# Transposes on the two halves of the TensorE array's rows in a fused encoder-decoder kernel

## The chip, the core and the metric

The kernel runs on one core of one Trainium2 chip. The metric is device time in microseconds (us) of one launch. Before the change three runs took 2826.58, 2827.00 and 2828.27 us; their median is 2827.0 us.

## The reference

A context of 77 rows goes through an encoder layer, and two sequences of 2048 rows go through a decoder layer (width 512, 16 heads of 32, hidden width 2048), all in fp32:

```
x = src
x = x + mha(ln(x), ln(x), ..., eb)
x = x + relu(ln(x) @ ff1.T + b1) @ ff2.T + b2
y = tgt
y = y + mha(ln(y), ln(y), ..., sb)        # causal, 2048 x 2048, 16 heads, two sequences
y = y + mha(ln(y), x, ..., cb)            # cross, 2048 x 77
y = y + relu(ln(y) @ ff1.T + b1) @ ff2.T + b2

scores = einsum('bhqd,bhkd->bhqk', q, k) / sqrt(32) + bias
attn = softmax(scores)
out = einsum('bhqk,bhkd->bhqd', attn, v)
```

The decoder's causal self-attention is most of the first 1745 us; the cross attention and the feed-forward layer of the decoder fill the rest.

## The kernel before

**Order.** Every engine has one queue, and each runs its instructions in the order in which the program emits them; there is no scheduler, the order is written out by hand. An engine that waits for a semaphore holds everything behind it.

**Units.** A unit is one sequence `b` (0, 1), one block `m` of 512 query rows (0 to 3), one group `g` of four heads (0 to 3) and one tile `t` of 128 rows (0 to 3): 128 units, in that order. Tile number `i = 4m + t` attends to `i + 1` key tiles, cut by `pieces` into pieces of two to four key tiles.

**One unit.** `scores` (L376) multiplies, for one piece, the four heads of the group on the four 32-row strips of the array, into four PSUM banks. VectorE copies each bank to SBUF and takes its maximum (L385; the diagonal with its bias, L392). After the last piece VectorE forms the negated maximum `nm` (L402), and the four exponentials of the unit, one for each head (ScalarE, L407), are put on a list, `late_exps`, from which `exps(k)` emits the next `k`. `turn` takes one or two pieces of a unit and transposes each 128x128 tile of the probabilities with TensorE (L428): four tiles to a PSUM bank, and one copy of that bank to the SBUF buffer `pts_all`. The first half of the banks of a turn is copied by ScalarE (L434), the second half by VectorE (L432); in the first block (m = 0) they take turns. After the fourth bank `turn` emits one exponential of a later unit, after the last another one. `values` (L445) multiplies the transposed tiles by V, on four column strips, into PSUM bank 7.

**The loop.** For each pair of pieces the main loop emits: the turn; after the last pair of a unit, `slot` (projections of q, k, v, the output projection, parts of the next block's normalization, here called jobs: L215, L226, L239, L251, each with eight matmuls over one bank; the transposes of a normalized tile, L308, and of the reciprocals of the softmax sums, L464); one piece of scores of a later unit, one to three exponentials; the values; and more scores where they may run ahead (up to two units).

**Banks.** `bank()` hands out seven PSUM banks in rotation. An operation that takes the n-th bank waits until the (n-7)-th has been read.

**Second part.** From 1745 us on eight blocks of 512 rows run through cross attention and feed-forward (matmuls L1323, L1352, L1424). There `bank()` rotates over four banks, `turned` of `attend_stages` transposes the 16 heads' probabilities of a tile (L814, four banks, ScalarE copies at L815), and `turned` of `norm_stages` four tiles of 128x128 (L759).

A matmul in fp32 stands in the trace as two passes, each with its weight load (PEld); a transpose as one. The lines that the steps below touch:

Of the kernel before, what the change touches and what calls it, by code (L numbers as in the profile page):

```python
# [11 lines left out]
AF = mybir.ActivationFunctionType  # L12
ALU = mybir.AluOpType
# [4 lines left out]
P = 128  # L18
B, T, S, D = 2, 2048, 77, 512
H, HD, DFF = 16, 32, 2048  # L20
NC = D // P
NF = DFF // P
HC = P // HD
MB = 512
NMB = T // MB
TB = MB // P
EPS = 1e-6
# [27 lines left out]
def tile_encoder_decoder(ctx: ExitStack, tc: tile.TileContext, ins, out):  # L55
    nc = tc.nc
    x, src = ins["x"], ins["ctx_1024"]
# [10 lines left out]
    ident = const.tile([P, P], F32, name="ident")  # L68
# [89 lines left out]
    with (  # L158
# [6 lines left out]
        kT = ac.tile([P, NC, T], F32, name="kT")  # L165
# [4 lines left out]
        nTt = ac.tile([P, NC, MB], F32, name="nT")  # L170
        wbt = ac.tile([P, NC, D], F32, name="wbig")
        pts_all = ac.tile([P, 8, HC * P], F32, name="pts")
        oT_all = ac.tile([P, 6, TB * P], F32, name="oT")
        bv = ac.tile([P, D], F32, name="row_sa_bv")
        bo = ac.tile([P, D], F32, name="row_dec_sa_out_b")
        psum = ps.tile([P, 8, 512], F32, name="psum")
        count = {"bank": 0, "banks": 7, "pts": 0, "oT": 0, "mm": 0}

        def bank():

            i = count["bank"] % count["banks"]
            count["bank"] += 1
            return psum[:, i, :]

        def in_turn(what, tile):
# [112 lines left out]
        def norm_turn(b, m, t, apart=False):  # L298
            xn = xs.pop((b, m, t))
            if t == 0:  # L300
                nTs[b, m] = nTt
            nT = nTs[b, m]

            pts = [bank()] * NC
            if apart:
                pts[0] = bank()
            for c in range(NC):
                nc.tensor.transpose(pts[c][:, ts(c, P)], xn[:, ts(c, P)], ident)  # L308
            for c in range(NC):
                d, pt = nT[:, c, ts(t, P)], pts[c]  # L310
                sc, bi = vec("dec_n1_s", c), vec("dec_n1_b", c)
                if c or not apart:
                    nc.scalar.activation(d, pt[:, ts(c, P)], AF.Identity, bias=bi, scale=sc)  # L313
                else:
                    nc.vector.tensor_scalar(d, pt[:, ts(c, P)], sc, bi, ALU.mult, ALU.add)


        def pieces(i):
# [15 lines left out]
        state = {}  # L334
# [78 lines left out]
        def turn(pieces):  # L413

            first = units[pieces[0][0]][1] == 0
            by_head = first or units[pieces[0][0]][2:] == (0, 0)
            loads = []
            for n, k0, kn in pieces:
                ks = range(k0, k0 + kn)
                if by_head:  # L420
                    loads += [[(n, k, r) for k in ks] for r in range(HC)]
                else:
                    loads += [[(n, k, r) for r in range(HC)] for k in ks]
            for o, load in enumerate(loads):
                pt = bank()
                pts = in_turn("pts", pts_all).rearrange("p (x q) -> p x q", q=P)
                for x, (n, k, r) in enumerate(load):
                    nc.tensor.transpose(pt[:, ts(x, P)], state[n]["p"][r][:, ts(k, P)], ident)  # L428
                    got[n, k, r] = pts[:, x, :]
                w = len(load) * P  # L430
                if o % 2 if first else o >= (len(loads) + 1) // 2:
                    nc.vector.tensor_copy(pts[:, : len(load), :], pt[:, :w])  # L432
                else:
                    nc.scalar.copy(pts[:, : len(load), :], pt[:, :w])  # L434
                if o == min(3, len(loads) - 1):
                    exps(1)
            exps(HC if first else 1)

# [14 lines left out]
        def divide(b, m, g):  # L453


            ri = sm.tile([P, TB, HC], F32, name="ri", tag="ri", bufs=2)
            nc.vector.reciprocal(ri, sums_of[b, m, g])
            rows = sm.tile([P, TB, HC, HD], F32, name="rirows", tag="rirows", bufs=1)
            nc.vector.tensor_copy(rows, ri[:, :, :, None].to_broadcast([P, TB, HC, HD]))
            yield  # L460
            rb = bank()
            flat = rows.rearrange("p t r d -> p (t r d)")
            for t in range(TB):
                nc.tensor.transpose(rb[:, ts(t, P)], flat[:, ts(t, P)], ident)  # L464
            nc.vector.tensor_tensor(ots[b, m, g], rb, ots[b, m, g], ALU.mult)
            yield


# [266 lines left out]
        def norm_stages(y, n, row, place, done):  # L735

            keep = {}

            def stats():
                st = sm.tile([P, 6], F32, name="bnst", tag="bnst")  # L740
                mv = sm.tile([P, 2], F32, name="cmv", tag="cmv", bufs=4)
                rs = sm.tile([P, 3], F32, name="crs", tag="crs", bufs=4)
                nc.vector.bn_stats(st, y())
                nc.vector.bn_aggr(mv, st)
                nc.vector.tensor_scalar_add(rs[:, 0:1], mv[:, 1:2], EPS)
                nc.gpsimd.tensor_tensor(rs[:, 1:2], rs[:, 0:1], mhalf[:, 0:1], ALU.pow)
                nc.gpsimd.tensor_scalar(rs[:, 2:3], mv[:, 0:1], rs[:, 1:2], -1.0, ALU.mult, ALU.mult)
                keep.update(rs=rs)

            def center():  # L750
                xn = keep["xn"] = place()
                rs = keep["rs"]
                nc.scalar.activation(xn, y(), AF.Identity, bias=rs[:, 2:3], scale=rs[:, 1:2])
                nc.gpsimd.tensor_tensor(y(), y(), row, ALU.add)

            def turned():
                xn, pt, dst = keep["xn"], bank(), done()
                for c in range(NC):
                    nc.tensor.transpose(pt[:, ts(c, P)], xn[:, ts(c, P)], ident)  # L759
                for c in range(NC):  # L760
                    sc, bi = vec(f"dec_{n}_s", c), vec(f"dec_{n}_b", c)
                    nc.scalar.activation(dst[:, c, :], pt[:, ts(c, P)], AF.Identity, bias=bi, scale=sc)

            return stats, center, turned

# [6 lines left out]
        def attend_stages(q, kTc, v, y, biased, pr, pts, place, w_o, bi=None):  # L772


            prh = pr.rearrange("p (h k) -> p h k", k=S)
            by_r = pr.rearrange("p (g r k) -> p g r k", r=HC, k=S)
            keep = {}
# [30 lines left out]
                nc.gpsimd.tensor_tensor(prh, prh, ri[:, :, None].to_broadcast([P, H, S]), ALU.mult)  # L808

            def turned():  # L810
                for g in range(NC):
                    pt = bank()
                    for r in range(HC):
                        nc.tensor.transpose(pt[:S, ts(r, P)], prh[:, g * HC + r, :], ident)  # L814
                    nc.scalar.copy(pts(g), pt[:S, :])  # L815

            def times_v():
                ot = bank()
                for g in range(NC):
                    for r in range(HC):  # L820
                        h = g * HC + r
                        nc.tensor.matmul(  # L822
                            ot[rows4(r), ts(g, P)], v[:, ts(h, HD)], pts(g)[:, ts(r, P)], start=True, stop=True
                        )
                keep["oT"] = place()
                nc.scalar.copy(keep["oT"], ot)
# [9 lines left out]
        def first_cross():  # L836
# [7 lines left out]
            o = 2 * HC * MB  # L844
# [13 lines left out]
            def pts(g):  # L858
                return kT[:S, g, 2 * MB : 3 * MB]

            def loads():
                for t in range(TB):
# [581 lines left out]
        def cross(x):  # L1444
# [26 lines left out]
            for t in range(TB):  # L1471
                at = 14 + 7 * t
                y = lambda t=t: y_of(x, t)
                biased = m == 0 and t < 2
                fs = attend_stages(
                    lambda g, t=t: qT[g // 2][:, g % 2, ts(t, P)], kTcs[b], vcs[b][:S, :], y, biased, pr,
                    lambda g: pts_all[:S, g, :], place("xr"), wbt,
                    bias_1 if biased and t else None,
                )
# [129 lines left out]
```

## Time and profile before

| | |
|---|---|
| median of the runs | 2827.0 us |
| the profiled execution, span | 2828.5 us |
| TensorE busy (matmul records) | 2796.6 us, 99% |
| VectorE busy | 1872.9 us, 66% |
| ScalarE busy | 1454.0 us, 51% |
| GpSimd busy | 787.9 us, 28% |
| transposes at L428 | 4352, 536.6 us |
| self-attention, by the first scores of each block | 24.4 to about 1745 us |

The span is that of one execution under the profiler. A row of the timeline gives the start, the length, the engine, the line and the operation, the output and the inputs, the shapes and the count, and in brackets how long the engine had been idle and what ended that. The end of a matmul is modelled with its way through the array, so a TensorE that is shown busy can still have gaps: what one transpose costs in a row of them is read from the length of the row and its count, not from the mean of one. The DMA queues' packets take 38% of the time of the 16 DMA engines.

### The profile page before, as it was taken

Reading aid. Unit: us, or ns where it says so; the run is one execution under the profiler, and the core shown is the slowest. Engines: PE = TensorE matmul, PEld = TensorE weight load, DVE = VectorE, ACT = ScalarE, POOL = GpSimd, SP = SyncE. Lnnn points to the kernel's source line nnn. Section 1 sums busy time; section 2 is a strip of 40 time slices with the busy share of each in tenths; the row PEclk is TensorE's granted clock in tenths of the full one; section 3 lists DMA queues with packets and bytes.
Section 4 is the critical chain, followed back from the end, with each engine's and each line's share of the span. In section 5 each row is a group of like instructions: output and inputs, shape, how many; then the busy total and the mean of one; then the engine's idle time right before and its main releaser. Section 6 shows DMA issues by size and latency. Waiting matters only on the chain.

```text
span 2828.5 us, 65166 instructions
## 1 busy us (share of the span) xinstructions
PE 2796.6 (99%) x25950; PEld 2062.6 (73%) x25950; DVE 1872.9 (66%) x5288; ACT 1454.0 (51%) x2785; POOL 787.9 (28%) x697
## 2 busy tenths in 40 slices
PE   9899999999999999999999999999999999999998
PEld 5557666666666556666666677888888888888888
DVE  4666687778887577687878895464645555555545
ACT  3544466656666556656656676434344444444431
POOL 0200050200000201120100002282828283837356
PEclk9999999999999999999999999999999999999999
DMA  6414343401111412332401014463637464646466
GB/s 172 122 33 130 119 137 103 125 17 46 34 44 58 120 48 61 80 102 68 124 20 32 21 60 144 135 216 116 205 120 207 138 197 127 194 131 187 125 201 194
DMA packets 252642, 319.10 MB, mean 113 GB/s; under 512 B 29568, under 2 KB 142512, under 8 KB 252210
## 3 DMA queue, kind: packets, MB, share of 16 engines
q1 hardware_dynamic: 252338, 314.93, 37.7%
q8 instruction: 205, 3.36, 0.5%
q14 instruction: 99, 0.81, 0.1%
HBM read 274.91 MB, written 39.95 MB: 111 GB/s over the span
## 4 chain that ended last, share of the span: by engine, by line
PE 93%; DVE 3%; ACT 1%; issue 1%; DMA 1%; POOL 1%; SPq 0%; POOLq 0%; ACTq 0%; DVEq 0%
PE psum L428 17%; PE psum L1323 14%; PE psum L1352 12%; PE psum L376 11%; PE psum L445 9%; PE psum L215 4%; PE psum L831 4%; PE psum L251 4%; PE psum L239 4%; PE psum L226 3%; PE psum L1424 3%; PE psum L814 2%; DVE pp L385 1%; PE psum L784 1%; PE psum L822 1%; PE psum L546 1%
## 5 line engine op out<-in xcount | busy, mean ns | idle before, releaser
L407 ACT ACTIVATE pp<-pp,nm 128x128 f32<-128x128 f32 (+15 forms) x512 | 612.7, 1204 | 219.7 <-DVE nm L402 219.2
L385 DVE TENSOR_SCALAR_CACHE_REDUCE pp<-psum 128x512 f32<-128x512 f32 (+3 forms) x1024 | 559.4, 591 | 61.7 <-PE psum L376 60.2
L428 PEld LDWEIGHTS psum<-ident,pp 128*128 128x128 f32 x4352 | 472.9, 141 | 111.8 <-DVE pp L385 53.1
L428 PE MATMUL psum<-ident,pp 128*128 128x128 f32 x4352 | 536.6, 277 | 9.2 <-ACT pp L407 2.8
L434 ACT COPY pts<-psum 128x512 f32<-128x512 f32 (+3 forms) x598 | 298.8, 571 | 437.6 <-PE psum L428 333.4
L432 DVE COPY pts<-psum 128x512 f32<-128x512 f32 (+3 forms) x556 | 330.8, 648 | 68.6 <-PE psum L428 68.5
L376 PE MATMUL psum<-kT,q 32*128 32x512 f32 (+3 forms) x2560 | 356.6, 576 | 6.0 <-ACT nT L313 2.7
L445 PEld LDWEIGHTS psum<-pts,vv 128*32 128x32 f32 x8704 | 226.0, 110 | 123.9 <-issue 116.0
L1352 PEld LDWEIGHTS psum<-pp 128*128 128x128 f32 x2560 | 295.8, 192 | 17.4 <-issue 12.8
L1352 PE MATMUL psum<-pp 128*128 128x128 f32 x2560 | 306.4, 276 | 1.9 <-POOL pp L1105 1.6
L445 PE MATMUL psum<-pts,vv 128*32 128x128 f32 x8704 | 278.8, 275 | 0.7 <-ACT pts L434 0.5
L1105 POOL TENSOR_TENSOR pp<-pp 128x512 f32<-128x512 f32 x155 | 209.5, 1368 | 111.7 <-DMA pp<-in_dec_ff_wT_dram 90.8
L1323 PE MATMUL psum<-vv,pp 128*128 128x256 f32 x1024 | 238.5, 381 | 0.0
L376 PEld LDWEIGHTS psum<-kT,q 32*128 32x128 f32 x2560 | 122.9, 183 | 141.2 <-issue 87.9
L1323 PEld LDWEIGHTS psum<-vv,pp 128*128 128x128 f32 x1024 | 189.8, 190 | 26.3 <-issue 1.9
L392 DVE CUSTOM_DVE_ANT_0 pp<-psum,bias 128x256 f32<-128x256 f32 (+1 forms) x512 | 196.0, 411 | 17.0 <-PE psum L376 17.0
L285 POOL TENSOR_TENSOR rstd<-rstd,mhalf 128x1 f32<-128x1 f32 x32 | 18.2, 569 | 659.1 <-DVE rstd L284 608.6
L1336 DVE TENSOR_TENSOR kT<-kT,psum 128x512 f32<-128x512 f32 x96 | 65.7, 685 | 181.0 <-PE psum L1323 181.0
L1339 ACT ACTIVATE kT<-kT,vecs 128x256 f32<-128x256 f32 x192 | 86.9, 500 | 168.7 <-DVE kT L1336 168.1
L1323 PE MATMUL psum<-nT,pp 128*128 128x256 f32 x768 | 173.4, 379 | 0.0
L1323 PEld LDWEIGHTS psum<-nT,pp 128*128 128x128 f32 x768 | 145.3, 190 | 22.6 <-issue 3.5
L808 POOL TENSOR_TENSOR oT<-oT,cri 128x1232 f32<-128x1232 f32 x28 | 67.7, 2416 | 283.4 <-DVE cri L803 258.4
(193 smaller groups left out, 3724.5 us busy)
## 6 DMA issues: line engine op xcount, KB each, us to landing
pp<-w_d SPq DMA_DIRECT2D x520, 256.0 KB, 2.9
pp<-in_dec_ff_wT_dram SPq DMA_DIRECT2D x112, 256.0 KB, 4.0
wqk<-in_dec_sa_in_wT_dram SPq DMA_DIRECT2D x64, 256.0 KB, 4.0
bias<-tzg SPq DMA_DIRECT2D x128, 128.0 KB, 3.8
wbig<-in_dec_sa_in_wT_dram SPq DMA_DIRECT2D x8, 1024.0 KB, 6.4
vv<-in_enc_ff_wT_dram SPq DMA_DIRECT2D x8, 1024.0 KB, 5.2
wbig<-in_dec_sa_out_wT_dram SPq DMA_DIRECT2D x8, 1024.0 KB, 6.4
vv<-y SPq DMA_DIRECT2D x32, 256.0 KB, 5.1
```

The lines of the kernel that those rows point to most:

```text
L215: nc.tensor.matmul(mm, w[:, c, :], nTs[b, m][:, c, :], start=(c == 0), stop=(c == NC - 1))
L376: nc.tensor.matmul(banks[r][:, : kn * P], q[rows4(r), ts(t, P)], kT[rows4(r), g, k0 * P : (k0 + kn) * P], start=True, stop=True,)
L385: nc.vector.tensor_scalar(p[:, k0 * P : (k0 + far) * P], s[:, : far * P], 1.0, None, ALU.mult, ALU.max, accum_out=st["mx"][:, r, c : c + 1],)
L392: nc.vector.tensor_tensor_reduce(p[:, (i + 1) * P - w : (i + 1) * P], s[:, far * P : kn * P], biases[b, m, g][:, r, 2 * P - w :], 1.0, LOW ...
L407: nc.scalar.activation(p, p, AF.Exp, bias=nm, accum_out=to)
L428: nc.tensor.transpose(pt[:, ts(x, P)], state[n]["p"][r][:, ts(k, P)], ident)
L432: nc.vector.tensor_copy(pts[:, : len(load), :], pt[:, :w])
L434: nc.scalar.copy(pts[:, : len(load), :], pt[:, :w])
L445: nc.tensor.matmul(ot[rows4(r), t, :], vv[:, k, ts(g * HC + r, HD)], got.pop((n, k, r)), start=(k == 0), stop=(k == i),)
L1105: engine.tensor_tensor(out, a, b, ALU.subtract)
L1323: nc.tensor.matmul(mm[:, ts(f, TOK)], a[:, c, ts(f, P)], b[:, c, :], start=fresh and f == 0 and c == 0, stop=c == 1, skip_group_check=True,)
L1352: nc.tensor.matmul(psum[:, bank_i, ts(col, P)], lhs[:, c, :], w[:, c, :], start=fresh and k in (0, 3) and c == 0, stop=c == 3, skip_group_ ...
```

## The change

`turn_halves` replaces each 128x128 transpose by two: rows 0 to 63 of the tile on the upper half of the array's rows and rows 64 to 127 on the lower half. Each streams 64 columns of the identity and writes 64 columns of the output, the one into a first bank, the other into a second. `two_banks` hands out two banks of the rotation. A pair of banks so holds eight tiles, each bank the halves of all eight. `turn` puts two of its former loads of four tiles into one group, and both engines copy of every group: ScalarE the first bank, VectorE the second, eight runs of 64 columns each. One exponential is now emitted after the second group. `pts_all` is used as a ring of 32 tiles, from its start again where a turn doesn't fit. All other transposes of the decoder (L308, L464, L759, L814) are changed in the same way; those of the encoder stay.

```diff
+        def two_banks():
+            n = count["bank"]
+            count["bank"] += 2
+            i, j = sorted((n % count["banks"], (n + 1) % count["banks"]))
+            return psum[:, i : j + 1 : j - i, :]
+
+        def turn_halves(pt, x, src, width=P):
+            for a in range(2):
+                rows = slice(a * HALF, (a + 1) * HALF)
+                nc.tensor.transpose(pt[:width, a, ts(x, HALF)], src[rows], ident[rows, rows])
...
-            for o, load in enumerate(loads):
-                pt = bank()
-                pts = in_turn("pts", pts_all).rearrange("p (x q) -> p x q", q=P)
+            groups = [sum(loads[o : o + 2], []) for o in range(0, len(loads), 2)]
+            if count["pts"] + sum(map(len, groups)) > pts_ring.shape[1]:
+                count["pts"] = 0
+            for o, load in enumerate(groups):
+                pt, w = two_banks(), len(load)
+                pts = pts_ring[:, count["pts"] : count["pts"] + w, :]
+                count["pts"] += w
                 for x, (n, k, r) in enumerate(load):
-                    nc.tensor.transpose(pt[:, ts(x, P)], state[n]["p"][r][:, ts(k, P)], ident)
+                    turn_halves(pt, x, state[n]["p"][r][:, ts(k, P)])
                     got[n, k, r] = pts[:, x, :]
-                w = len(load) * P
-                if o % 2 if first else o >= (len(loads) + 1) // 2:
-                    nc.vector.tensor_copy(pts[:, : len(load), :], pt[:, :w])
-                else:
-                    nc.scalar.copy(pts[:, : len(load), :], pt[:, :w])
-                if o == min(3, len(loads) - 1):
+                for a, copy in enumerate((nc.scalar.copy, nc.vector.tensor_copy)):
+                    copy(
+                        pts[:, :, ts(a, HALF)], pt[:, a, : w * HALF].rearrange("p (x q) -> p x q", q=HALF)
+                    )
+                if o == min(1, len(groups) - 1):
                     exps(1)
             exps(HC if first else 1)
...
             def turned():
-                for g in range(NC):
-                    pt = bank()
-                    for r in range(HC):
-                        nc.tensor.transpose(pt[:S, ts(r, P)], prh[:, g * HC + r, :], ident)
-                    nc.scalar.copy(pts(g), pt[:S, :])
+                for g in range(0, NC, 2):
+                    pt = two_banks()
+                    for x in range(2 * HC):
+                        turn_halves(pt, x, prh[:, g * HC + x, :], S)
+                    d = pts.rearrange("p g (r a q) -> p g r a q", r=HC, a=2)[:, g : g + 2]
+                    for a in range(2):
+                        nc.scalar.copy(
+                            d[:, :, :, a, :], pt[:S, a, :].rearrange("p (g r q) -> p g r q", g=2, q=HALF)
+                        )
```

More of the change, by code (lines that the diff above doesn't have):

```diff
@@ L23 @@
 HC = P // HD
+HALF = P // 2
 MB = 512
@@ L302, in norm_turn @@
             nT = nTs[b, m]
-            pts = [bank()] * NC
+            pts = [two_banks()] * NC
             if apart:
-                pts[0] = bank()
+                pts[0] = two_banks()
             for c in range(NC):
-                nc.tensor.transpose(pts[c][:, ts(c, P)], xn[:, ts(c, P)], ident)
+                turn_halves(pts[c], c, xn[:, ts(c, P)])
             for c in range(NC):
-                d, pt = nT[:, c, ts(t, P)], pts[c]
+                d, pt = joined(nT[:, c, ts(t, P)]), pts[c][:, :, ts(c, HALF)]
                 sc, bi = vec("dec_n1_s", c), vec("dec_n1_b", c)
                 if c or not apart:
-                    nc.scalar.activation(d, pt[:, ts(c, P)], AF.Identity, bias=bi, scale=sc)
+                    nc.scalar.activation(d, pt, AF.Identity, bias=bi, scale=sc)
                 else:
-                    nc.vector.tensor_scalar(d, pt[:, ts(c, P)], sc, bi, ALU.mult, ALU.add)
+                    nc.vector.tensor_scalar(d, pt, sc, bi, ALU.mult, ALU.add)
         def pieces(i):
@@ L460, in divide @@
             yield
[L461 removed]
+            rb = two_banks()
             flat = rows.rearrange("p t r d -> p (t r d)")
             for t in range(TB):
[L464 to L465 removed]
+                turn_halves(rb, t, flat[:, ts(t, P)])
+            o = ots[b, m, g].rearrange("p (t a q) -> p a t q", t=TB, a=2)
+            nc.vector.tensor_tensor(
+                o, rb[:, :, : TB * HALF].rearrange("p a (t q) -> p a t q", q=HALF), o, ALU.mult
+            )
             yield
@@ L756, in turned @@
             def turned():
-                xn, pt, dst = keep["xn"], bank(), done()
+                xn, pt, dst = keep["xn"], two_banks(), done()
                 for c in range(NC):
-                    nc.tensor.transpose(pt[:, ts(c, P)], xn[:, ts(c, P)], ident)
+                    turn_halves(pt, c, xn[:, ts(c, P)])
                 for c in range(NC):
                     sc, bi = vec(f"dec_{n}_s", c), vec(f"dec_{n}_b", c)
-                    nc.scalar.activation(dst[:, c, :], pt[:, ts(c, P)], AF.Identity, bias=bi, scale=sc)
+                    nc.scalar.activation(
+                        joined(dst[:, c, :]), pt[:, :, ts(c, HALF)], AF.Identity, bias=bi, scale=sc
+                    )
             return stats, center, turned
@@ L822, in times_v @@
                         nc.tensor.matmul(
-                            ot[rows4(r), ts(g, P)], v[:, ts(h, HD)], pts(g)[:, ts(r, P)], start=True, stop=True
+                            ot[rows4(r), ts(g, P)], v[:, ts(h, HD)], pts[:, g, ts(r, P)], start=True, stop=True
                         )
```

9 lines of the change are left out of this document (6 added, 3 removed).

## The prediction

> **What bounds the kernel now.** I read the page first, then the table by stage, then the timeline of one turn in each kind of block.
>
> ```profile
> span 2828.5 us, 65166 instructions
> PE 2796.6 (99%) x25950; PEld 2062.6 (73%) x25950; DVE 1872.9 (66%) x5288; ACT 1454.0 (51%) x2785; POOL 787.9 (28%) x697
> ...
> PE 93%; DVE 3%; ACT 1%; issue 1%; DMA 1%; POOL 1%; SPq 0%; POOLq 0%; ACTq 0%; DVEq 0%
> ...
> L428 PE MATMUL psum<-ident,pp 128*128 128x128 f32 x4352 | 536.6, 277 | 9.2 <-ACT pp L407 2.8
> ```
>
> TensorE holds 93% of the chain of waits, and the transposes are 536.6 us of it. That share is an average. By stage, the last block of the first sequence (m = 3) reads:
>
> ```profile
> core 0: us, PE busy (x) PEld busy (x) DVE busy (x) ACT busy (x) POOL busy (x), PEclk, DMA share, GB/s
> 604.10:887.10 283.00, 281.19 (x3361) 191.34 (x3360) 238.99 (x745) 186.91 (x268) 8.17 (x12) 1.00 0.14 41
> ```
>
> VectorE is busy for 239.0 of 283.0 us (84%) there: TensorE leads, with VectorE close behind. One iteration of that block (a turn of 32 tiles, scores, values, scores, a turn of 20):
>
> ```profile
> 701.14 3.71 PE L428 MATMUL psum<-ident,pp 128*128 128x128 f32 x32
> 701.75 0.42 DVE L392 CUSTOM_DVE_ANT_0 pp<-psum,bias 128x256 f32<-128x256 f32 x1
> 701.83 2.05 ACT L434 COPY pts<-psum 128x512 f32<-128x512 f32 x4 [6.97 <-DVE oT L451]
> 703.24 0.17 DVE L402 TENSOR_REDUCE nm<-mx 128x4 f32<-128x16 f32 x1
> 703.58 2.48 DVE L432 COPY pts<-psum 128x512 f32<-128x512 f32 x4 [0.17 <-PE psum L428]
> 703.75 1.82 ACT L407 ACTIVATE pp<-pp,nm 128x1792 f32<-128x1792 f32 x1
> 704.78 0.31 PEld L376 LDWEIGHTS psum<-kT,q 32*128 32x128 f32 x8 [0.17 <-issue]
> 704.78 1.14 PE L376 MATMUL psum<-kT,q 32*128 32x512 f32 x8
> 705.53 1.80 ACT L407 ACTIVATE pp<-pp,nm 128x1792 f32<-128x1792 f32 x1
> 705.85 1.95 PE L445 MATMUL psum<-pts,vv 128*32 128x128 f32 x64
> 708.81 2.40 PE L428 MATMUL psum<-ident,pp 128*128 128x128 f32 x20
> 708.89 0.69 DVE L385 TENSOR_SCALAR_CACHE_REDUCE pp<-psum 128x512 f32<-128x512 f32 x1 [0.39 <-PE psum L376]
> 710.73 0.69 DVE L385 TENSOR_SCALAR_CACHE_REDUCE pp<-psum 128x512 f32<-128x512 f32 x1
> 711.48 0.30 PEld L215 LDWEIGHTS psum<-nT,wqk 128*128 128x128 f32 x2
> ```
>
> See that ScalarE copied its four banks at 701.83 while VectorE was still emptying score banks (until 703.2), and that the exponential came after them: the first half of a turn's banks came free early.
>
> **The transposes.** 32 take 3.71 us, of which 0.277 is the way of the last: (3.71 - 0.28)/31 = 0.11 us each. What a narrower one takes is seen in the encoder:
>
> ```profile
> 40.00 0.70 PE L534 MATMUL psum<-ident,pp 77*128 77x77 f32 x8
> 125.67 1.27 PE L593 MATMUL psum<-ident,pp 77*77 77x77 f32 x16
> ```
>
> Eight with 128 weight columns and 77 streamed: (0.70 - 0.23)/7 = 0.067 us; with 77 weight columns (1.27 - 0.23)/15 = 0.069. So the pace follows the streamed columns, and 64 should take about 0.055. That the two halves run side by side is supported by the scores above: eight matmuls of 512 columns on 32-row strips take 1.14 us, where eight on the full array (L831 in the next fence) take 3.60. I take 0.055 for a pair (between 0.055 and 0.11, if they don't overlap), 0.069 where the tile is 77 wide (L814): 4864 x 0.054 + 512 x 0.040 = 283 us of TensorE time less.
>
> **The switches.** A group in another tiling starts after 0.17 to 0.20 us of idle weight load (704.78), while L215 after L428 shows none. The new half-row form makes every passage to a full-array matmul a switch. About 90 jobs follow a turn directly: 90 x 0.20 = 18 us. In the second part L814 runs 28 times and L759 56 times between full-array matmuls:
>
> ```profile
> 1845.59 1.91 PE L814 MATMUL psum<-ident,oT 128*77 128x128 f32 x16
> ...
> 1837.25 0.60 PE L759 MATMUL psum<-ident,xt 128*128 128x128 f32 x4
> ...
> 1838.58 3.60 PE L831 MATMUL psum<-wbig,xr 128*128 128x512 f32 x8
> ```
>
> A visit costs 0.15 + 0.20 us of switches. L814 saves 16 x 0.040 = 0.64, net -0.29 x 28 = -8 us; L759 saves 0.22, net +0.13 x 56 = +7. The second part: **-1 us**; its copies are as many as before and hidden by full-array matmuls.
>
> The Trainium skill, TensorEngine Tiling (Array Packing), Key Properties, says that a change of tiling mode drains TensorE; the 0.17 to 0.20 us above agree, and by that rule none of the 84 visits goes without the two switches.
>
> **The copies.** As many elements as before, about 600 copies on each engine. Eight runs of 64 instead of one of 512 I price by the nearest strided row:
>
> ```profile
> L794 DVE TENSOR_TENSOR oT<-psum,cmx 128x308 f32<-128x308 f32 x104 | 49.8, 479 | 5.0
> L432 DVE COPY pts<-psum 128x256 f32<-128x256 f32 x36 | 13.1, 416 | 1.1 <-PE psum L428 1.1
> L432 DVE COPY pts<-psum 128x384 f32<-128x384 f32 x24 | 12.1, 549 | 1.0 <-PE psum L428 1.0
> ```
>
> Between 416 and 549 ns a contiguous copy of 308 columns would take 470; the four strided runs take 479. So 0 to 0.02 us a copy, taken as zero, covered by the waits below; uncovered 600 x 0.02 = 12 us.
>
> **What the new grouping waits for.** Call the groups of a turn G1 to G4, t = 0 its start. Two things change. Every group now needs VectorE, which begins with the backlog of score banks; and the exponential now stands in ScalarE's queue between G2 and G3, so that G3 and G4 wait for nm and for it. TensorE's next scores take the four banks after the turn's eight, of seven: VectorE's of G1, both of G2, and ScalarE's of G3.
>
> *m = 3, turn at 701.14.* nm at 2.27; G1 and G2 on ScalarE by 2.1; exponential 2.3 to 4.1 (cadence 705.53 - 703.75); G3 0.51 later (four in 2.05), 4.6. The scores' last strip starts there and takes 0.96 (1.14 less the way through the array); they end at 5.6 instead of 4.62: **+1.0 us**, though the transposes themselves end a microsecond earlier. Second turn (708.81): VectorE empties the last score bank 2.5 after its start (708.89 to 711.4); with the pair of banks for L464 between, the job waits for VectorE's copy of G1 behind that, 3.1, plus 0.15 for weights: 3.25 instead of 2.67, **+0.6**.
>
> ```profile
> 718.27 3.90 PE L428 MATMUL psum<-ident,pp 128*128 128x128 f32 x32
> 721.06 0.17 DVE L402 TENSOR_REDUCE nm<-mx 128x4 f32<-128x20 f32 x1
> 721.27 1.90 ACT L407 ACTIVATE pp<-pp,nm 128x1920 f32<-128x1920 f32 x1 [0.25 <-DVE nm L402]
> ...
> 754.37 3.71 PE L428 MATMUL psum<-ident,pp 128*128 128x128 f32 x32
> 755.96 0.17 DVE L402 TENSOR_REDUCE nm<-mx 128x4 f32<-128x16 f32 x1
> ```
>
> The unit at 718.27: nm at 2.96, G3 at 5.4, +1.6, second turn -0.1. That at 754.37: nm at 1.76, G3 at 4.0, +0.35, second turn (32 tiles) -0.4. The fourth kind has a still later nm and +1.7. Mean of the four kinds +1.2 us. Of 32 units 28 have scores behind the first turn: +34; four have none and keep 1.5 each: -6. **+28 us.**
>
> ```profile
> 489.46 3.71 PE L428 MATMUL psum<-ident,pp 128*128 128x128 f32 x32
> 490.50 1.26 ACT L407 ACTIVATE pp<-pp,nm 128x1152 f32<-128x1152 f32 x1 [2.34 <-DVE nm L402]
> 491.75 2.02 ACT L434 COPY pts<-psum 128x512 f32<-128x512 f32 x4
> 493.10 1.86 PE L376 MATMUL psum<-kT,q 32*128 32x512 f32 x8
> ...
> 267.76 3.71 PE L428 MATMUL psum<-ident,pp 128*128 128x128 f32 x32
> 269.35 0.16 DVE L402 TENSOR_REDUCE nm<-mx 128x4 f32<-128x8 f32 x1
> 271.75 3.60 PE L251 MATMUL psum<-wbig,oT 128*128 128x512 f32 x8
> ```
>
> *m = 2.* At 489.46 one exponential already stood ahead and the scores waited for ScalarE even before (1.86 us). After: copies from 2.3, second exponential 3.4 to 4.6, G3 at 5.2, scores end at 6.1 against 5.3: +0.8. Three of four kinds are so; small second turns give back 0.3 to 0.4 or lose 0.3 to a bank of the scores. The fourth has no exponential there and gains 0.6. Mean +0.3 x 32 = **+10**. *m = 1.* A job follows the turn and needs VectorE's bank of G1, or, where another pair of banks (L308) stands between, that of G2: in the last rows, with statistics on VectorE ahead of its copies, 4.0 instead of 3.99. With nothing between it would start there at 2.5 instead of 3.55; with a backlog a microsecond longer it starts later than before. These cancel: **+2**. *m = 0*: few tiles, **-3**.
>
> Sum: 2828.5 - 3 + 2 + 10 + 28 - 1 = 2864.5 against the profiled execution, which stands 1.5 above the median: **2863 us**.
>
> **The rivals.** (A) *The exponential doesn't hold G3*, because ScalarE gets it early enough or the backlog of VectorE melts as TensorE arrives earlier. Then VectorE's half of G2 decides: m = 3 comes to 0 and the four tails' -6, m = 2 to -13, the rest as above: 2828.5 - 21 - 1.5 = **2806**. It ends on the other side; the point is 0.25 us a unit over 60 units, where I have 0.9. For it: ScalarE is busy for 187 of 283 us only. Against: nm, which it must wait for, comes late in each row shown. (B) *TensorE's saving goes through*: 283 - 18 - 29 = 236 us, **2591**. For: 93% of the chain. Against: VectorE's 239 of 283 us and the rotation of banks. (C) *The halves are no faster than the whole*, 0.11 us a pair: m = 3 +41, m = 2 +26, m = 1 +10, m = 0 +6, second part 84 x 0.35 = +29: **2939**. The Trainium skill, TensorE: Matmul & The Clock Gate, LDWEIGHTS, says that a weight load takes the columns over 1.2 (in ns), whatever the rows; by it a half of 128 columns needs 107 ns and C holds. The 0.067 us of L534, with 128 columns, speak against it for transposes.
>
> **Chances.** Forecast 0.48 (its own range 2835 to 2895), C 0.10, slower copies or more 0.04; A 0.22; B, whole or in part, 0.12; within 0.2% 0.04 (about what a measurement of this kernel tells from no change). Slower 0.62, faster 0.34. From 2770 to 2940 lie the forecast, A, about half of C and the near ones: 0.8.
>
> **What would show it.** Right: pairs of halves at about 0.055 us; turns with long gaps inside; the scores after a turn waiting for ScalarE's copy behind an exponential; TensorE's busy share down while the span isn't. Wrong: scores that follow the transposes within 0.2 us, or a VectorE that is busy throughout m = 3.

## The result and the profile after

The changed kernel takes 2983.0 us (four runs, 2980.8 to 2999.0) against 2827.6 us: a ratio of 1.056, interval 1.054 to 1.059. It is 155 us slower; the prediction had 36 us slower and a range that ended at 2940. The profiled execution is the slowest of the four, 2999.0 us with a span of 2997.2, so what is read from it stands 16 us above the median.

The page of the changed kernel, busy time of the engines and the group of half transposes:

```profile
span 2997.2 us, 76055 instructions
...
PE 2815.9 (94%) x31326; PEld 1952.9 (65%) x31326; DVE 1885.6 (63%) x5330; ACT 1457.8 (49%) x2785; POOL 786.4 (26%) x697
...
L198 PE MATMUL psum<-ident,pp 64*128 64x64 f32 (+1 forms) x8848 | 407.2, 231 | 80.4 <-DVE mx L411 27.7
```

VectorE and ScalarE do what they did (1885.6 against 1872.9 us, 1457.8 against 1454.0). TensorE's share fell from 99 to 94%, and the transposes now wait 80 us in all where they waited 9. The table by stage, for the blocks m = 0 to 3 of the first sequence and then of the second (columns as in the prediction: stretch, its length, busy time of TensorE, weight loads, VectorE, ScalarE, GpSimd, then the granted clock):

```profile
29.40:169.20 139.80, 125.75 (x1117) 69.43 (x1116) 83.02 (x324) 62.06 (x191) 15.72 (x16) 0.93 0.41 113
169.20:389.10 219.90, 205.18 (x2340) 133.00 (x2339) 141.21 (x489) 102.34 (x210) 25.96 (x28) 0.97 0.30 93
389.10:644.40 255.30, 234.47 (x3234) 138.36 (x3233) 185.72 (x595) 144.27 (x236) 49.86 (x48) 0.95 0.35 101
644.40:966.50 322.10, 295.36 (x4308) 177.94 (x4307) 241.55 (x752) 189.22 (x270) 8.19 (x12) 0.95 0.12 36
966.50:1116.30 149.80, 135.97 (x1329) 72.80 (x1328) 87.47 (x327) 72.09 (x214) 18.73 (x25) 0.95 0.33 89
1116.30:1331.80 215.50, 191.90 (x2401) 111.16 (x2400) 140.44 (x469) 122.56 (x249) 23.43 (x28) 0.93 0.21 60
1331.80:1588.50 256.70, 236.24 (x3233) 138.40 (x3232) 186.05 (x595) 144.41 (x237) 33.07 (x32) 0.94 0.25 75
1588.50:1903.90 315.40, 290.26 (x4561) 181.09 (x4560) 241.79 (x747) 183.94 (x257) 8.89 (x7) 0.96 0.14 42
```

The block m = 3 that took 283.0 us now takes 322.1, with the same 239 to 242 us of VectorE. The lengths of the same eight stretches before were 137.1, 208.5, 234.1, 283.0, 145.1, 189.7, 233.9 and 286.5 us. In all: start +5, m = 0 +7, m = 1 +37, m = 2 +44, m = 3 +68, second part +7, which is the 169 us between the two spans.

One turn of m = 2 and what follows it, from the timeline of the changed kernel:

```profile
450.71 1.77 PE L198 MATMUL psum<-ident,pp 64*128 64x64 f32 x49
...
451.74 1.25 ACT L426 ACTIVATE pp<-pp,nm 128x1152 f32<-128x1152 f32 x1 [4.11 <-DVE nm L421]
...
453.00 1.05 ACT L454 COPY pts<-psum 128x512 f32<-128x512 f32 x2
...
453.62 0.70 PE L198 MATMUL psum<-ident,pp 64*128 64x64 f32 x15 [1.13 <-ACT pts L454]
453.94 1.26 ACT L426 ACTIVATE pp<-pp,nm 128x1152 f32<-128x1152 f32 x1
...
454.25 1.14 PE L395 MATMUL psum<-kT,q 32*128 32x512 f32 x6
...
455.19 1.06 ACT L454 COPY pts<-psum 128x512 f32<-128x512 f32 x2
...
455.82 2.06 PE L395 MATMUL psum<-kT,q 32*128 32x512 f32 x2 [0.44 <-ACT pts L454]
...
457.81 3.64 PE L467 MATMUL psum<-pts,vv 128*32 128x128 f32 x64
```

This turn has the form of the one that the prediction worked out for m = 2 (32 tiles, exponentials of 1152 columns, one of them ahead of the copies). The prediction had ScalarE's copies from 2.3 us after the start (453.00 - 450.71 = 2.29), the second exponential from 3.4 to 4.6 (3.2 to 4.5), and the copy of G3 done at 5.2 (the last strip of the scores starts at 5.1). What it did not have comes next: the 64 matmuls of the values take 3.64 us; in the kernel before, the same 64 took 1.95 (at 435.17 there). The same place by windows of 3.4 us:

```profile
449.10:452.50 3.40, 3.38 (x82) 2.54 (x81) 3.08 (x12) 0.76 (x1) 0.00 (x0) 1.00 0.57 152
452.50:455.90 3.40, 1.85 (x22) 0.95 (x22) 2.18 (x4) 3.40 (x8) 0.00 (x0) 1.00 0.67 158
455.90:459.30 3.40, 3.40 (x30) 1.79 (x34) 2.13 (x8) 2.83 (x5) 0.00 (x0) 0.50 0.01 3
459.30:462.70 3.40, 3.40 (x51) 2.10 (x40) 0.00 (x0) 0.00 (x0) 0.00 (x0) 0.50 0.00 0
462.70:466.10 3.40, 3.32 (x40) 2.02 (x37) 2.92 (x9) 1.17 (x2) 0.00 (x0) 1.00 0.02 5
```

After a window in which TensorE had work for 1.85 of 3.4 us, its granted clock is 0.50 for two windows. In the second of these VectorE and ScalarE do nothing at all: they wait for a TensorE at half its pace. The chip thus charges for waits that the prediction counted at their own length only. The trace of the changed kernel has 41 such stretches, of 3.4 us (22 of them), 6.8 (18) and 10.2 (1). If the whole trace is cut into windows of 3.41 us that start where the clock changes, all 20 windows at full clock in which TensorE's records cover less than 0.6 of the time are followed by half clock; of those with 0.6 to 0.9 it is 19 of 132, of those with more 2 of 665. Over the whole run the mean granted clock fell from 0.996 to 0.966; as the windows show 1.00 or 0.50, that is 2 x 0.034 x 2997 = 204 us at half clock, against some 23 before.

The Trainium skill, TensorE: Matmul & The Clock Gate, describes such an effect in "A second HAM failure mode: psum-queue depth-cycling": a TensorE that idles briefly and often between groups of matmuls, as it cycles through PSUM banks, has its clock throttled again and again. These rows agree. Its section "HAM oscillation" states the rule as no idle gaps over about 3.4 us; the gaps here are 1.13 and 0.44 us, inside one window, and the clock fell after them.

### The profile page after: what moved, and what is told of

It is laid out like the page before. It is cut to its first block, busy times and chain, and to the rows that moved or that the text cites. A ratio compares the mean times of both kernels' runs of the same rounds, so it can differ in the third digit from the quotient of the medians.

```text
span 2997.2 us, 76055 instructions
## 1 busy us (share of the span) xinstructions
PE 2815.9 (94%) x31326; PEld 1952.9 (65%) x31326; DVE 1885.6 (63%) x5330; ACT 1457.8 (49%) x2785; POOL 786.4 (26%) x697
## 5 line engine op out<-in xcount | busy, mean ns | idle before, releaser
L454 ACT COPY pts<-psum 128x512 f32<-128x512 f32 (+3 forms) x598 | 308.3, 545 | 570.1 <-PE psum L198 540.2
L198 PE MATMUL psum<-ident,pp 64*128 64x64 f32 (+1 forms) x8848 | 407.2, 231 | 80.4 <-DVE mx L411 27.7
L198 PEld LDWEIGHTS psum<-ident,pp 64*128 64x128 f32 (+1 forms) x8848 | 339.7, 141 | 208.3 <-DVE pp L404 64.0
L395 PE MATMUL psum<-kT,q 32*128 32x512 f32 (+3 forms) x2560 | 429.5, 585 | 21.2 <-ACT pts L454 9.7
L454 DVE COPY pts<-psum 128x512 f32<-128x512 f32 (+3 forms) x598 | 346.3, 633 | 38.2 <-PE psum L198 23.8
L467 PEld LDWEIGHTS psum<-pts,vv 128*32 128x32 f32 x8704 | 240.8, 115 | 135.4 <-issue 125.8
L467 PE MATMUL psum<-pts,vv 128*32 128x128 f32 x8704 | 299.4, 288 | 3.3 <-ACT pts L454 2.9
L395 PEld LDWEIGHTS psum<-kT,q 32*128 32x128 f32 x2560 | 145.5, 187 | 196.4 <-issue 77.4
L270 PE MATMUL psum<-wbig,oT 128*128 128x512 f32 x256 | 143.6, 713 | 17.0 <-ACT pp L787 7.6
```

The lines of the kernel that those rows point to most:

```text
L198: nc.tensor.transpose(pt[:width, a, ts(x, HALF)], src[rows], ident[rows, rows])
L270: nc.tensor.matmul(mm, ots[b, m, c][:, ts(t, P)], w[:, c, :], start=(c == 0), stop=(c == NC - 1))
L395: nc.tensor.matmul(banks[r][:, : kn * P], q[rows4(r), ts(t, P)], kT[rows4(r), g, k0 * P : (k0 + kn) * P], start=True, stop=True,)
L454: copy(pts[:, :, ts(a, HALF)], pt[:, a, : w * HALF].rearrange("p (x q) -> p x q", q=HALF))
L467: nc.tensor.matmul(ot[rows4(r), t, :], vv[:, k, ts(g * HC + r, HD)], got.pop((n, k, r)), start=(k == 0), stop=(k == i),)
```

## The experiments

In the expectations, G is the prediction's mechanism: what the new grouping of the copies makes TensorE wait for. H is the rival that the half transposes themselves cost it, by more instructions, more changes of tiling, or a clock that sees less work. Where a time at half clock is given, it is worked out from the mean granted clock as above.

**The grouping alone, with whole transposes.** From the kernel before: two loads make a group over two banks, ScalarE copies the first bank, VectorE the second, and the exponential comes after the second group; each tile is still transposed whole.

```diff
-            for o, load in enumerate(loads):
-                pt = bank()
+            groups = [sum(loads[o : o + 2], []) for o in range(0, len(loads), 2)]
+            for o, load in enumerate(groups):
+                pt, w = two_banks(), len(load)
+                h = (w + 1) // 2
...
-                    nc.tensor.transpose(pt[:, ts(x, P)], state[n]["p"][r][:, ts(k, P)], ident)
+                    nc.tensor.transpose(pt[:, x // h, ts(x % h, P)], state[n]["p"][r][:, ts(k, P)], ident)
...
+                for a, copy in enumerate((nc.scalar.copy, nc.vector.tensor_copy)):
+                    m = min(h, w - a * h)
+                    copy(pts[:, a * h : a * h + m, :], pt[:, a, : m * P])
-                if o == min(3, len(loads) - 1):
+                if o == min(1, len(groups) - 1):
                     exps(1)
```

> The kernel before, with the new grouping alone: whole 128x128 transposes, two banks to a group of eight tiles, ScalarE copies the first bank and VectorE the second, the exponential after the second group. Theory G: the waits are there without any half-row transpose, the clock drops less because TensorE is busier: 2870 to 2930 us. Rival H: as before, 2820 to 2835 us.

2892.2 us, ratio 1.023 (1.0215 to 1.0245): +65 us without a single half transpose and with a mean clock of 0.996. H alone, with a time as before, is out. The groups of TensorE in m = 3 of the first sequence, the kernel before first:

```profile
L376 PE MATMUL psum<-kT,q 32*128 32x512 f32 (+2 forms) x512 | 71.0, 599 | 0.4 <-DVE pp L385 0.3
```

and this kernel, with its row by stage:

```profile
L384 PE MATMUL psum<-kT,q 32*128 32x512 f32 (+2 forms) x512 | 85.4, 599 | 1.9 <-ACT pts L445 1.4 <-DVE pp L393 0.5
```

```profile
613.10:918.60 305.50, 297.32 (x3361) 196.67 (x3360) 242.79 (x752) 189.36 (x268) 8.17 (x12) 1.00 0.12 37
```

The same scores occupy TensorE 14 us longer although one of them takes 599 ns in both: their strips start apart instead of together. Of the 1.9 us that TensorE stood idle ahead of them, 1.4 ended with ScalarE's copy. By blocks m = 1 loses 9 us, m = 2 12 and m = 3 43.

**The same, with the exponential after the last group.**

```diff
-                if o == min(1, len(groups) - 1):
+                if o == len(groups) - 1:
                     exps(1)
```

> The new grouping with whole transposes, the exponential after the last group. If the exponential ahead of G3 is what the grouping costs (65 us), most of it goes: 2830 to 2850 us. If VectorE's half of every group is what costs, it stays: 2870 to 2892 us.

2850.4 us, 1.0081 (1.0066 to 1.0096). The exponential ahead of G3 is 42 of the 65 us. The other 23 go with what still differs from the kernel before, VectorE's part in every group and banks taken by twos; no run separates these.

**The exponential last, in the changed kernel.** The same edit there.

> The changed kernel, but the exponential in the middle of a turn is emitted after the last group, not after the second. Theory G (the loss of 155 us comes from the new grouping: every group needs VectorE, G3 and G4 stand behind an exponential, and the waits let the granted clock drop): G3's copy by ScalarE no longer waits, the forecast's +1.2 us a unit at m = 3 and +0.8 at m = 2 go, and part of the half-clock time (209 us in the profile) with them: 2880 to 2930 us. Rival H (the half-row transposes themselves cost it: more instructions, more changes of tiling, a clock that sees less work): no change, 2970 to 2990 us.

2920.5 us, 1.033 (1.031 to 1.035): 63 us come back, with a mean clock of 0.972. As G had it. The same edit is worth 42 us where TensorE keeps its clock and 63 here.

**The copies in their old order.** Changed kernel, but the two copies of a group go to one engine: ScalarE the first half of the groups, VectorE the second.

```diff
-                for a, copy in enumerate((nc.scalar.copy, nc.vector.tensor_copy)):
+                for a in range(2):
+                    copy = nc.scalar.copy if 2 * o + a < len(groups) else nc.vector.tensor_copy
                     copy(
```

> The changed kernel, but the banks of a turn are dealt to the engines as before: of the copies of a turn ScalarE takes the first half, VectorE the second, whatever half of the tiles they hold. Theory G: the first banks come free without VectorE and nothing of ScalarE's stands behind the exponential, so half of TensorE's saving of 236 us or more remains: 2650 to 2790 us, with a clock near 0.99. Rival H: 2900 us or more.

2888.8 us, 1.0218 (1.0203 to 1.0233), clock 0.976: 94 us come back, but not TensorE's saving. By G the halves without the new order of copies should have come to 2650 to 2790 us; this is where G, as the whole story, fell. The time lies 62 us above the kernel before and just below H's range (2900 or more). The block m = 3 takes 285.5 us, as before, with TensorE idle for 19 of them and VectorE at work for 240.

**More copies on ScalarE.** If VectorE holds the turns, it should help to give ScalarE three quarters of the copies and to put the exponential last.

```diff
+                    copy = nc.scalar.copy if 2 * (2 * o + a) < 3 * len(groups) else nc.vector.tensor_copy
...
-                if o == min(1, len(groups) - 1):
+                if o == len(groups) - 1:
```

> Half-row transposes, the copies of a turn dealt in order with three quarters on ScalarE, the exponential after the last group. Theory V (with the transposes halved VectorE is the bound of m = 2 and m = 3: dealt in order the blocks m = 3 take 286 us, as before, with VectorE busy for 239): VectorE loses a quarter of its copies, about 150 us over the kernel, and the m = 3 blocks fall below 275 us; in all 2780 to 2870 us. Rival: ScalarE, with a quarter more copies and the exponentials, becomes late: m = 3 at 286 us or more, 2889 us or more.

2926.8 us, 1.034 (1.033 to 1.036): 38 us worse than the old order; the expected gain failed. In m = 3 of the first sequence VectorE works for 206 us instead of 240, ScalarE for 218 instead of 187, and the block takes 296.0 instead of 285.4 us. The half transposes there:

```profile
L198 PE MATMUL psum<-ident,pp 64*128 64x64 f32 x1824 | 84.0, 230 | 18.7 <-DVE pp L404 7.6 <-DVE mx L411 6.1 <-ACT pts L455 3.5
```

They still wait, and mostly for VectorE to empty a score bank, though VectorE has less to do. So the amount of VectorE's work is not what holds the turns. That a late ScalarE costs the 38 us is likely but not shown: the run changes the share and the place of the exponential at once.

**The same share in the kernel before**, with whole transposes.

```diff
-                if o % 2 if first else o >= (len(loads) + 1) // 2:
+                if o % 2 if first else o >= (3 * len(loads) + 3) // 4:
...
-                if o == min(3, len(loads) - 1):
+                if o == (min(3, len(loads) - 1) if first else (3 * len(loads) + 3) // 4 - 1):
```

> The kernel before (whole transposes) with three quarters of a turn's copies on ScalarE, the exponential after the last of them. Control for the run with halves: if TensorE bounds the kernel before, shifting copies brings nothing: 2820 to 2840 us. If VectorE did, it is faster, 2780 to 2810.

2833.4 us, 1.002 (1.001 to 1.003): nothing to be had there.

**Every half transpose in a turn twice.**

```diff
-                    turn_halves(pt, x, state[n]["p"][r][:, ts(k, P)])
+                    for _ in range(2):
+                        turn_halves(pt, x, state[n]["p"][r][:, ts(k, P)])
```

> The changed kernel with each half-row transpose of a turn done twice, to the same place: 8704 more of them, some 4352 x 0.062 = 270 us of TensorE work, no other wait. Theory C (the granted clock falls to one half because the turns' waits leave TensorE idle for much of a few microseconds; half of the 181 us that TensorE is busy at half clock in the profile, some 81 us more than before, is lost that way): the waits are filled with work, the half-clock time falls from 209 us towards the 23 us of whole transposes, and the time falls to about 2892 us, that of the new grouping with whole transposes, between 2880 and 2930. Rival N (the clock isn't what costs): 2983 us or more, up to 2983 + 270.

3031.3 us, 1.072 (1.070 to 1.074), clock 0.986. The expectation of a time below the changed kernel's, by a clock that stays up, failed. The time lies in the range of rival N, that the clock isn't what costs. But 4352 more pairs of some 0.06 us each, 270 us of work, cost only 48. The block m = 3 of this kernel, by stage and by groups:

```profile
658.00:980.00 322.00, 313.75 (x6132) 219.09 (x6131) 244.78 (x752) 188.80 (x268) 8.18 (x12) 0.98 0.12 37
```

```profile
L198 PE MATMUL psum<-ident,pp 64*128 64x64 f32 x3648 | 127.1, 226 | 3.0 <-DVE pts L455 2.0 <-ACT pts L455 0.6
```

and the group of the changed kernel in its 322.1 us:

```profile
L198 PE MATMUL psum<-ident,pp 64*128 64x64 f32 x1824 | 85.2, 231 | 19.1 <-DVE mx L411 6.3 <-DVE pp L404 5.9 <-DVE pts L454 2.7
```

Twice the transposes fit into the same 322 us. In the changed kernel the turn stands for 19 us, mostly until VectorE has emptied a score bank; doubled, it stands for 3. A part of the room comes from the clock, 0.98 here against 0.95 (some 10 us, half of the difference at half clock). Most of the time that a half transpose saves on TensorE is thus not on the path there: TensorE would wait for banks instead.

**Halves in the cross attention and its norm alone**, all else as before.

> The kernel before, with half-row transposes in the cross attention alone (norm and probabilities there, about 770 of 5376 tiles), self-attention as before. The prediction's term for the second part: -1 us. Theory G: 2822 to 2835 us. Rival H: an eighth of the loss or more, 2845 us upwards.

2841.6 us, 1.005 (1.003 to 1.007): +15 us against the runs of the kernel before beside it (2826.8), where the prediction's term was -1. Half of it is in the second part (from the transposes of the last reciprocals, 1749.32 before and 1753.66 here, to the end of the span: 1079.2 and 1086.2 us), half in the block m = 0 of the second sequence, which already holds such work (145.1 to 152.6 us between first scores). Visits of the norm's transposes between output projections, before:

```profile
1756.66 0.60 PE L759 MATMUL psum<-ident,xt 128*128 128x128 f32 x4
1757.10 3.60 PE L251 MATMUL psum<-wbig,oT 128*128 128x512 f32 x8
1760.53 0.60 PE L759 MATMUL psum<-ident,xt 128*128 128x128 f32 x4
```

and in this kernel:

```profile
1761.10 0.46 PE L197 MATMUL psum<-ident,xt 64*128 64x64 f32 x8
1761.49 3.70 PE L269 MATMUL psum<-wbig,oT 128*128 128x512 f32 x8
1765.12 0.46 PE L197 MATMUL psum<-ident,xt 64*128 64x64 f32 x8
...
1769.14 0.46 PE L197 MATMUL psum<-ident,pts 64*128 64x64 f32 x8
1771.69 5.40 PE L269 MATMUL psum<-wbig,oT 128*128 128x512 f32 x8 [2.09 <-ACT pp L780]
```

An ordinary visit costs 4.02 instead of 3.87 us, +0.15 (the prediction: +0.13). The step was sized rightly; the surplus is elsewhere. The third projection waits 2.09 us for ScalarE and then runs at a granted clock of 0.68 (5.40 us instead of 3.70): 3.8 of the 7 us in one place.

**Pairs of neighbouring banks only.** That wait has a cause in the program. `two_banks` goes round with the rotation, so some pairs consist of the first and the last bank. One instruction that reads both (the norm's activations L332 and L787, the division L488) is ordered in the program as if it read the banks between them as well. The changed kernel, timeline:

```profile
526.77 1.28 DVE L454 COPY pts<-psum 128x512 f32<-128x512 f32 x2
528.14 1.51 ACT L332 ACTIVATE nT<-psum,vecs 128x128 f32<-128x128 f32 x4 [2.80 <-DVE pts L454]
529.70 2.08 PE L270 MATMUL psum<-wbig,oT 128*128 128x512 f32 x2 [3.95 <-ACT nT L332]
```

L332 here reads the first and the seventh bank; it waits for VectorE's copy of the sixth, and the output projection, which writes the second, waits for L332. The view of what TensorE waited for ahead of L270, over the run (us, times):

```profile
  ACT pp L787: 15.5, 4
  ACT nT L332: 13.3, 4
```

The edit skips the last bank where a pair would begin with it:

```diff
-            n = count["bank"]
+            if (count["bank"] + 1) % count["banks"] == 0:
+                count["bank"] += 1
+            i = count["bank"] % count["banks"]
             count["bank"] += 2
-            i, j = sorted((n % count["banks"], (n + 1) % count["banks"]))
-            return psum[:, i : j + 1 : j - i, :]
+            return psum[:, i : i + 2, :]
```

> Changed kernel, but a pair of banks is always two neighbours: where the next bank is the seventh, it is skipped, so that no pair consists of the first and the seventh. In the changed kernel four output jobs (L270) start 4.75, 6.3, 3.4 and 2.6 us late, each behind a read of such a pair by one instruction (the norm's activations or the division) although they write another bank; and the first scores start 5 us later than before. Theory that an instruction that reads the first and the seventh bank is ordered against everything between them: the four waits go and the start comes back by some 4 us, 15 to 25 us in all, 2950 to 2970 us. Rival, that these waits are the engines' own queues: 2975 to 2995 us, and the output jobs still wait.

> The kernel with the copies in their old order (2889 us) and neighbours as pairs. Theory of the first-and-seventh pair: 15 to 25 us less, 2864 to 2874 us. Rival, that the late jobs only move another wait: 2880 to 2895 us. Neither gives a time below the kernel before.

In the kernel with the copies in their old order: 2867.2 us, 1.0137 (1.0122 to 1.0152), 22 us less, as the theory had it; the first scores start at 23.7 us instead of 29.2, and the mean clock rises from 0.976 to 0.980. In the changed kernel itself: 2977.0 us, with runs from 2955.9 to 2981.8, a gain of 6 us, inside the rival's range and no more than the spread of these runs, although the two kinds of wait are gone; what TensorE waited for ahead of the output projection there:

```profile
  issue: 54.4, 201
  DVE pts L455: 3.2, 11
```

Its clock stayed at 0.968. So it is shown that such pairs cause these waits. To remove them is worth 22 us in the one kernel and no clear gain in the other; that other waits take the time again there is likely, not shown.

**Work in TensorE's waits.** Six whole transposes behind each turn of m = 1 to 3, into the bank that the next instruction takes; 160 x 6 x 0.11 = 105 us and about 32 us of switches.

```diff
+            n, k, r = load[-1]
+            if units[n][1]:
+                spare = psum[:, count["bank"] % count["banks"], :P]
+                for _ in range(6):
+                    nc.tensor.transpose(spare, state[n]["p"][r][:, ts(k, P)], ident)
             exps(HC if first else 1)
```

In the changed kernel:

> Changed kernel with more work for TensorE: behind each turn of the blocks m = 1 to 3, six whole 128x128 transposes into the bank that the next instruction takes (160 x 6, about 105 us of TensorE's time at 0.109 us each, and some 32 switches); what they write is overwritten. They lie where TensorE waits for ScalarE's copy before the next scores. Theory that the lowered granted clock is a cost of its own, brought on by these waits: half-clock time falls from 209 us to 60 to 130 us, and the time stays at or below the changed kernel's in spite of the work, 2920 to 2985 us. Rival, that the lowered clock lies only where TensorE waits anyway: 3000 to 3085 us.

and in the kernel with the old order and neighbouring pairs:

> Old order of copies, neighbours as pairs, and the same six transposes behind each turn. Theory that the lowered clock costs by itself: half-clock time falls below 80 us and the time lies within 15 us of the same kernel without the added work, 2850 to 2885 us. Rival, that it lies in waits only: 50 to 100 us above that kernel.

3004.9 us (1.063; 1.061 to 1.064) and 2944.2 us (1.040; 1.038 to 1.043). The spans and mean clocks of the changed kernel, of it with the added work, of the old order with neighbouring pairs, and of that with the added work:

```profile
core 0: 2997.2 us, clock 0.966
```

```profile
core 0: 3002.5 us, clock 0.980
```

```profile
core 0: 2865.5 us, clock 0.980
```

```profile
core 0: 2943.4 us, clock 0.981
```

The same work costs 22 us in the changed kernel, where the time at half clock falls by 84 us (204 to 120), and 77 us in the other, where it stays (115 to 112). If lost clock cost half its length, the first would have been given 42 us back, and the work would have cost 64 there. That fits, but it isn't proof: TensorE also stands idle longer in m = 1 to 3 of the changed kernel (132 us, the six lengths less TensorE's busy time in the table above) than in the other (89 us), and so has more room for such work. Both times lie in the rival's ranges, since the added work was dearer than what came back. What the lowered clock costs by itself is therefore bounded, not measured. At most it is half of 204 us, less the 12 it cost before, 90 us. For the other end the trace of the changed kernel gives an estimate: in 54 of the us at half clock TensorE works while VectorE, ScalarE and GpSimd all stand idle, as in the window at 459.30; before, that was 1 us. There nothing but TensorE's pace sets the time, and at full clock these stretches would be half as long: some 27 us.

No version with halves came below the kernel before; the nearest with all of them is the 2867.2.

## Why the prediction was wrong

The direction was right, and so were the turns that the prediction worked out; the sum was not. It priced the new waits at their own length with a granted clock that stays up, and the clock did not. Block by block the terms (forecast, measured) are: start 0 and +5 us, m = 0 -3 and +7, m = 1 +2 and +37, m = 2 +10 and +44, m = 3 +28 and +68, second part -1 and +7. By its steps:

- **Pairs of halves.** Predicted 0.055 us; (1.77 - 0.23)/24 = 0.064 us in the row at 450.71. Rival C (0.11) is out. The rule of the Trainium skill, TensorE: Matmul & The Clock Gate, LDWEIGHTS, that the prediction weighed (by it an estimated 107 ns for 128 columns) doesn't set the pace of these transposes. The switches (0.15 + 0.20 us) held: the visit shown came to +0.15 where +0.13 was forecast.
- **Copies.** Priced at no change; right: a copy of 256 columns takes 415 ns on VectorE, as it did (416).

```profile
L454 DVE COPY pts<-psum 128x256 f32<-128x256 f32 x70 | 28.0, 415 | 5.2 <-PE psum L198 2.6 <-ACT pts L454 1.8 <-ACT pp L426 0.7
```

- **What the new grouping waits for.** This is the step that the runs bear out: the grouping alone costs 65 us, the exponential ahead of G3 42 of them. The same turns in the changed kernel (at 748.93, 767.72 and 812.09 us, and at 514.09 for m = 2; matched by the count of score matmuls ahead of them) end their scores 1.05, 1.66 and 0.45 us later than before, where the prediction had +1.0, +1.6 and +0.35 for m = 3, and 0.74 for the turn of m = 2, where it had +0.8. The turns that it did not work out, and m = 1 above all, whose terms it let cancel, came to more: with whole transposes, at full clock, m = 3 is +43 and m = 1 +9.
- **The clock.** This is the step that was missing. The table of before showed a granted clock of 0.99 to 1.00 in m = 1 to 3, and the sum took that for given while it put gaps of a microsecond into every turn. With halves, TensorE's work in a turn is shorter and its waits longer; windows fall to half use, and the next one or two run at half clock. What that does to work that waits for nobody shows in the output projections of m = 3, in the kernel before and in the changed one:

```profile
L251 PE MATMUL psum<-wbig,oT 128*128 128x512 f32 x32 | 14.4, 592 | 0.0
```

```profile
L270 PE MATMUL psum<-wbig,oT 128*128 128x512 f32 x32 | 19.2, 755 | 0.0
```

  The jobs and the values of both blocks m = 3, the same matmuls, take 210 us of TensorE's time before, 209 with the grouping alone and 232 in the changed kernel. From the kernel with the grouping alone (2892) to the changed one (2983) there are 91 us more, although TensorE has some 190 us less to do (4864 pairs by 0.046 and 512 by 0.031, less 47 us of switches). The start, the second part and the first-and-last pairs show a part of them; how much of the rest is the clock stays open within the bounds above.
- **The second part, -1 us.** It became +7. The visits were right; the late projection behind a first-and-last pair was not foreseen. Nor was the start, +5, which went with neighbouring pairs (first scores at 25.7 us in the changed kernel with them). The wait on banks that aren't read could have been found in the order of the program's waits before any run.
- **Rival A** (the exponential doesn't hold G3) is refuted by the 42 and 63 us of the two kernels that move it. **Rival B** (TensorE's saving goes through) is refuted by the old order (2888.8) and by the doubled transposes. Of the prediction's reasons against B, the rotation of banks agrees with what the doubled kernel waits for; VectorE's 239 of 283 us does not hold as a bound, since the run with more copies on ScalarE took VectorE's work away and m = 3 became longer. What keeps the kernel with 2867.2 us from using TensorE's saving stays open: its clock was 0.980, and in m = 1 to 3 TensorE stood idle for 89 us.

## What to carry to other kernels

An engine that is busy for 99% need not be worth relieving: look at what it will wait for in the same stage when its own work is shorter, and test it by doubling the work that is to be saved; if the time hardly moves, so will the saving. Before a change that puts short waits into a TensorE that never waited, price its clock as well: here each window at about half use was followed by one or more at half pace. A pair of resources from a rotation should never be its last and its first, if one instruction reads both.

## What was not expected of the hardware

Gaps of 1.13 and 0.44 us in one stretch of 3.4 us were followed by 6.8 us at half clock; no long idle time was needed. And the two kernels with the lowest clock here vary more: the runs of the changed kernel (0.966) spread over 18 us and those with neighbouring pairs (0.968) over 26, where those of the kernel before lie within 3 to 6. It is no rule: the kernel with the old order and neighbouring pairs (0.980) spreads over 2.
